# Attention probabilities turned by block transposes and a trip through DRAM instead of TensorE, in a two-layer gated cross-attention network

## The chip, the cores and the metric

The kernel runs on one core of a Trainium2 chip (TensorE for matrix products, VectorE, ScalarE, GpSimd, SyncE which issues DMAs). The metric is device time in microseconds of one launch. Everything is float32 except a bfloat16 mask bias.

## The reference

`x` is (8, 512, 512): 8 batches of 512 tokens, 512 features. The context is (8, 120, 512): 120 keys a batch. There are 16 heads of 32 features. Two layers, each a gated cross-attention and a gated feed-forward:

```python
def xattn(Q, ctx, Wq, Wk, Wv, Wo, mask=None):      # layer 1 adds biases and a key mask
    q, k, v = split_heads(Q @ Wq.T), split_heads(ctx @ Wk.T), split_heads(ctx @ Wv.T)
    scores = einsum('bhqd,bhkd->bhqk', q, k) / sqrt(32)
    if mask is not None:
        scores = where(mask == 0, -1e30, scores)
    probs = softmax(scores)                        # (8, 16, 512, 120)
    out = einsum('bhqk,bhkd->bhqd', probs, v)
    return merge_heads(out) @ Wo.T

x = x + tanh(g_xattn[0]) * xattn(layernorm(x), ctx, ...)
x = x + tanh(g_ffn[0]) * routed_ffn(layernorm(x))  # 128 experts, each takes 1 token of each 32
x = x + tanh(g_xattn[1]) * xattn(layernorm(x), ctx, ..., mask)
x = x + tanh(g_ffn[1]) * channel_mix(layernorm(x)) # two mixes with the previous token, 3 products
```

## The kernel before

The 4096 tokens are 32 tiles of 128 tokens (`NT = 32`, `TB = 4` tiles a batch). `x` stays on the chip. Both cross-attentions are the class `CrossAttention`; the work is a software pipeline of slots, one for each tile. `slot(t)` does, in program order:

- `normalize(t + 10)`: layernorm of a later tile by ScalarE; in layer 1 GpSimd also adds the output bias (`add_bias`).
- `scores(t + 1)`: 16 products (one a head) of queries and keys into two PSUM tiles `s` of 8 heads (in layer 1 first four products that add the mask), then the softmax. The heads of `s[1]` go one at a time through ScalarE: VectorE takes the largest of each head (line 674), and eight activations compute exp(s - max) and the sum of each head (677). The heads of `s[0]` go together: VectorE takes the largest (685) and subtracts it (687), one wide activation does the exponentials (688), VectorE sums (693). `norm` takes reciprocals (666) and divides on GpSimd (667), for 8 heads at a time.
- `queries`: two of the seven products that make a later batch's queries (each four matmuls, line 156; the seventh alone in every fourth slot), with their copies and sums on ScalarE, VectorE and GpSimd. I call the slot with one product the short slot.
- `output(t - 1, ...)`: the output projection of the tile before, in two parts (757), and the update of `x` (766).
- `transpose_probs(t)`: 16 TensorE transposes of the probabilities, [128 tokens, 120 keys] to [120 keys, 128 tokens] (705), into PSUM, then two copies to `prT` on the chip, one by VectorE (713), one by ScalarE (715).
- `transpose_x(t + 9)`: four transposes of a normalised tile (567) and a ScalarE copy (569).
- `attend(t)`: 16 products of values and `prT` (740), then the copy `aT` by ScalarE (748).

At the marks `after(t, stage)` the next part of the network puts its own work in: in layer 0 the routing of the feed-forward (`RoutedFfn.in_slot`: statistics, `route_norm` with a copy of `x` to DRAM and a ScalarE normalisation, `route_x`, `route_logits`), in layer 1 the statistics and, from slot 22 on, the first work of the channel mix (`ChannelMix.in_slot`). Slots 0 to 3 are the opening; `run` does slots 4 to 26; `tail` slots 27 to 32, which use `transpose_probs_late`.

What sets the order: inside `tc.manual_schedule(engines=...)` the named engines take their instructions in program order; the other engines are ordered by the framework's scheduler. In `run`, layer 0 has only TensorE in program order, layer 1 TensorE and SyncE. SyncE's queue takes DMAs in order, and a DMA that waits holds those behind it. On-chip tiles come from pools: `soft` (two buffers a name; `pr` are the probabilities, 128 x 2048), `late` (`prT`, one buffer), PSUM pools `p_s` (two buffers of two banks: the two `s` tiles or `tps`) and `p_mm` (four banks, shared in turn by query products, attention, routing, transposed x and output).

Of the kernel before, what the change touches and what calls it, by code (L numbers as in the profile page):

```python
# [28 lines left out]
EPS = 1e-5  # L29

MASKED = -(2.0**102)


class Common:
# [172 lines left out]
class CrossAttention:  # L207
# [7 lines left out]
    def __init__(  # L215
        self, cm, tc, es, ins, gate, aside, mask=None, biases=None, loads=(), then=None,
        vpool=None,
    ):
        self.cm, self.nc, self.tc, self.gate, self.then = cm, cm.nc, tc, gate, then
        self.masked, self.biased = mask is not None, biases is not None  # L220

        self.aside, self.turned = aside, not loads
        nc = cm.nc

        def pool(name, bufs, **kw):
            pool = tc.tile_pool(name=name, bufs=bufs, reuse_waits="tile", **kw)
            return es.enter_context(pool)

        self.pool = pool("at_w", 1)
        vpool = vpool or self.pool  # L230
        self.norm = pool("at_n", 2)
        self.soft = pool("at_soft", 2)
        self.p_mm = pool("at_mm", 4, space=PSUM)
        self.p_s = pool("at_s", 2, space=PSUM)
        self.wq = self.pool.tile([P, NC, D], FP, name="wq")
        self.wo = self.pool.tile([P, NC, D], FP, name="wo")
        self.kT = self.pool.tile([P, NC, B * LK], FP, name="kT")
        self.v = [vpool.tile([P, 2, D], FP, name=f"v{q}") for q in range(B // 2)]
        self.xn, self.xnT, self.qT, self.probs, self.aT = {}, {}, {}, {}, {}
        self.ops = {}  # L240
        self.biasless, self.opening = [], True

        def right(name):
            return tc.tile_pool(name=name, bufs=1, side="right", reuse_waits="tile")

        with right("at_v") as self.vp:
            with right("at_k") as self.kp:
                self.load(ins, list(loads), mask, biases)
                if self.biased:
                    self.scale_biases()  # L250
                self.project_keys()
                if self.masked:
                    self.make_mask()
            self.work = pool("at_work", 2)
            self.prologue()
        self.late = pool("at_late", 2)
# [359 lines left out]
    def queries(self, b, f):  # L616

        if f == 0:
            self.begin_queries(b)
        one = f == TB - 1 or self.opening and f == 2  # L620
        self.q7.next(1 if one else 2)
        if f == 0:
            self.sum_tokens(2)

    def scores(self, t):

        nc, soft = self.nc, self.soft  # L630
        b, i = divmod(t, TB)
        toks = slice(i * P, (i + 1) * P)
        keys = slice(b * LK, (b + 1) * LK)
# [12 lines left out]
        for hc in range(NC):  # L646
            for j in range(4):
                r = 32 * j
                nc.tensor.matmul(  # L649
                    s[j // 2][:, j % 2, hc * LK : (hc + 1) * LK],  # L650
                    self.qT[b][r : r + 32, hc, toks],
                    self.kT[r : r + 32, hc, keys],
                    start=not self.masked,
                    stop=not self.masked or hc == NC - 1,
                )
        pr = soft.tile([P, NC * S], FP, name="pr")[:, : NH * LK]
        pr = pr.rearrange("p (j h k) -> p j h k", h=NC, k=LK)
        sm = soft.tile([P, 4, NC], FP, name="sm")
        sv = [
            s[u][:, :, : NC * LK].rearrange("p j (h k) -> p j h k", k=LK) for u in range(2)  # L660
        ]
        rs = soft.tile([P, 4, NC, 1], FP, name="rs")

        def norm(js):
# [5 lines left out]
            )  # L670


        nmx = soft.tile([P, 2, NC, 1], FP, name="nmx")
        nc.vector.tensor_reduce(nmx, sv[1], AX.X, ALU.max, negate=True)  # L674
        for j in range(2):
            for hc in range(NC):
                nc.scalar.activation(  # L677
                    pr[:, 2 + j, hc, :],
                    sv[1][:, j, hc, :],
                    AF.Exp,  # L680
                    bias=nmx[:, j, hc, :],
                    accum_out=sm[:, 2 + j, hc : hc + 1],
                )
        mx = soft.tile([P, 2, NC, 1], FP, name="mx")
        nc.vector.tensor_reduce(mx, sv[0], AX.X, ALU.max)  # L685
        pv = pr[:, :2, :, :]
        nc.vector.tensor_tensor(pv, sv[0], mx.to_broadcast([P, 2, NC, LK]), ALU.subtract)  # L687
        nc.scalar.activation(pv, pv, AF.Exp)  # L688
        self.probs[t] = pr

# [3 lines left out]
            lambda: norm(slice(0, 2)),  # L694
        ]

    def transpose_probs(self, t):
        nc = self.nc
        pr = self.probs.pop(t)
        prT = self.late.tile([P, 4, NC, P], FP, name="prT", bufs=1)[:LK]  # L700
        for u in range(2):
            ps = self.p_s.tile([LK, 2, NC * P], FP, name="tps", tag="s")
            for jj in range(2):
                for hc in range(NC):
# [2 lines left out]
                        pr[:, 2 * u + jj, hc, :],  # L707
                        self.cm.ident,
                    )
            dst = prT[:, 2 * u : 2 * u + 2, :, :]  # L710
            src = ps.rearrange("p j (h t) -> p j h t", t=P)
            if u == 0:
                nc.vector.tensor_copy(dst, src)  # L713
# [4 lines left out]
    def transpose_probs_late(self, t):  # L718

        nc = self.nc  # L720
        pr = self.probs.pop(t)
        prT = self.late.tile([P, 4, NC, P], FP, name="prT", bufs=1)[:LK]
        for j in (2, 3, 0, 1):
            ps = self.p_mm.tile([LK, NC, P], FP, name="tps", tag="mm")
            for hc in range(NC):
                nc.tensor.transpose(ps[:, hc, :], pr[:, j, hc, :], self.cm.ident)
            if j % 2 == 0:
                nc.vector.tensor_copy(prT[:, j, :, :], ps)  # L728
            else:
                nc.scalar.copy(prT[:, j, :, :], ps)  # L730
        self.probs[t] = prT

    def attend(self, t):
# [3 lines left out]
        for hc in range(NC):  # L737
            for j in range(4):
                h = 4 * hc + j
                nc.tensor.matmul(  # L740
                    aps[32 * j : 32 * j + 32, hc, :],
                    self.v[b // 2][:LK, b % 2, h * HD : (h + 1) * HD],
                    prT[:, j, hc, :],
                    start=True,
                    stop=True,
                )
        self.aT[t] = self.late.tile([P, NC, P], FP, name="aT")
        nc.scalar.copy(self.aT[t], aps)  # L748

    def output(self, t, chunks):  # L750

        nc, x = self.nc, self.cm.x
        if 0 in chunks:
            self.ops[t] = self.p_mm.tile([P, D], FP, name="ops", tag="mm")
        ops = self.ops[t]
# [6 lines left out]
                stop=(c == NC - 1),  # L762
            )
        if NC - 1 in chunks:
            del self.ops[t], self.aT[t]
            nc.vector.scalar_tensor_tensor(
                x[:, t, :], ops, self.gate, x[:, t, :], ALU.mult, ALU.add
            )

    def after(self, t, stage):  # L770

# [3 lines left out]

    def run(self):
        for t in range(TB, NT - TB - 1):
            self.slot(t)

    def slot(self, t):  # L780

        if t + 10 < NT and not self.opening:
            self.normalize(t + 10)
        rest = self.scores(t + 1)
        while rest and not self.opening:
            rest.pop(0)()
        self.queries(*divmod(t + TB + 1, TB))
        self.after(t, 0)


        short = t % TB == TB - 2
        ahead = 3 if short or t == 1 else 2
        if t > 0:
            self.output(t - 1, range(ahead))
        x_ahead = short and not self.masked and not self.opening
        if x_ahead and t + 9 < NT:
            self.transpose_x(t + 9)
        if rest:
            rest.pop(0)()
        self.transpose_probs(t)  # L800
        while rest:
            rest.pop(0)()
# [2 lines left out]
            self.q7.next()  # L805
        if t > 0:
            self.output(t - 1, range(ahead, NC))
        if t + 9 < NT and not x_ahead:
            self.transpose_x(t + 9)
        if self.opening:  # L810
            self.add_bias(2)
            self.normalize(t + 10)
        self.after(t, 1)
        self.attend(t)
        self.after(t, 2)

    def tail(self):

        for t in range(NT - TB - 1, NT + 1):
            rest = self.scores(t + 1) if t + 1 < NT else []  # L820
            self.after(t, 3)
            self.after(t, 0)
# [11 lines left out]
class RoutedFfn:  # L834
# [43 lines left out]
    def route_stats(self, t):  # L878
        layernorm_sums(self.cm, self.route, t)
        layernorm_scales(self.cm, self.route, t, 1)  # L880

    def route_norm(self, t):

        nc, x = self.nc, self.cm.x[:, t, :]
        nc.sync.dma_start(out=self.aside[t * P : (t + 1) * P, :], in_=x)
        nc.scalar.activation(
            x, x, AF.Identity, bias=self.cm.nmr[:, t, :], scale=self.cm.rstd[:, t, :]
        )

    def route_x(self, t, ps):  # L890
        nc = self.nc
# [36 lines left out]
    def in_slot(self, s, attention, stage):  # L928

        last = NT - TB - 1  # L930
        if stage == 2 and 0 <= s - 1:
            self.route_stats(s - 1)
        if (stage == 2 and (0 <= s - 1 < last - 1 or s == NT)) or (stage == 3 and s > last):
# [269 lines left out]
class ChannelMix:  # L1203
# [56 lines left out]
    def in_slot(self, s, attention, stage):  # L1260

        nc = self.nc
        self.at = attention
        if stage == 2 and 0 <= s - 2 < NT - 2 * TB:
            attention.stats(s - 2)
        if stage == 2 and s == NT - 1:
            for c in range(NC):
# [256 lines left out]
def flamingo_kernel(ctx: ExitStack, tc: tile.TileContext, a: dict, out: bass.AP):  # L1524
# [25 lines left out]
    with ExitStack() as es:  # L1550
# [5 lines left out]
        with ExitStack() as at:  # L1556
            with tc.manual_schedule(engines=every):
# [3 lines left out]
                    vpool=ffn.vpool,  # L1561
                )
                attention.first_slots()
            with tc.manual_schedule(engines={engines.PE}):
                attention.run()
            with tc.manual_schedule(engines=compute):
                attention.tail()
# [1 line left out]
    with ExitStack() as es:  # L1569
# [3 lines left out]
        with tc.manual_schedule(engines=every):  # L1573
# [2 lines left out]
                gates[:, 1:2], aside, a["mask"], (a["bqk"], a["bv"], a["bo"]), then=mix.in_slot,  # L1576
            )
            attention.first_slots()
        with tc.manual_schedule(engines={engines.PE, engines.SP}):
            attention.run()  # L1580
        with tc.manual_schedule(engines=compute):
            attention.tail()
# [64 lines left out]
```

## Time and profile before

| | |
|---|---|
| median of 3 runs | 1404.27 us (1403.76 to 1408.66) |
| the profiled execution | span 1402.0 us, from its first to its last instruction |
| TensorE matmul busy | 1363.8 us, 97% |
| VectorE, ScalarE, GpSimd busy | 1051.7 (75%), 761.8 (54%), 698.9 us (50%) |
| DMA | 71.45 MB in 46010 packets, nearly all in the loads at the start and in the feed-forward of layer 0 |
| the chain that ended last, by engine | TensorE 71%, VectorE 15%, ScalarE 5%, GpSimd 5% |

The slots of layer 0 run from about 85 to 410 us, those of layer 1 from about 750 to 1045 us. The chain is the sequence of work that ended last: each piece was waited for by the next. A group's row gives the line, the engine, the operation, the tile written and the tiles read, shapes, count, busy time, mean duration of one, and the idle time of the engine just before it with what ended it. `PEld` is TensorE's weight load, which runs beside its products.

### The profile page before, as it was taken

How to read it: one execution, taken by the hardware profiler on the slowest of the kernel's cores; microseconds unless marked ns; L12 is line 12 of the kernel's file. 1: busy time of each engine (PE TensorE's matmuls, PEld its weight loads, DVE VectorE, ACT ScalarE, POOL GpSimd, SP SyncE). 2: the span in 40 equal slices, each digit the busy share in tenths (PEclk: the TensorE clock that was granted, in tenths of full speed). 3: DMA queues.
4: the chain of work that ended last, by engine and by line, in shares of the span. 5: the costliest groups of instructions: out<-in, count | busy, mean ns of one | idle time of the engine just before them, and what ended most of it. 6: DMA issues, size and time to landing. Idle time of an engine off the chain costs nothing.

```text
span 1402.0 us, 32996 instructions
## 1 busy us (share of the span) xinstructions
PE 1363.8 (97%) x13888; PEld 1099.8 (78%) x13888; DVE 1051.7 (75%) x1498; ACT 761.8 (54%) x1860; POOL 698.9 (50%) x620
## 2 busy tenths in 40 slices
PE   7999999999999998999999999999999999999997
PEld 6887777777777787888888777777766888888886
DVE  4876767777777777777887777777777678877776
ACT  1366666666666445445136666665665655544543
POOL 4855545555444001555797766565548244343341
PEclk9999999999999999999999999999999999999999
DMA  9500000000001347431410000000000000000001
GB/s 297 184 8 25 17 23 24 24 24 24 18 30 47 130 133 240 123 107 61 148 61 2 2 1 2 1 2 2 1 32 2 0 31 30 31 31 31 30 22 40
DMA packets 46010, 71.45 MB, mean 51 GB/s; under 512 B 2926, under 2 KB 22894, under 8 KB 45862
## 3 DMA queue, kind: packets, MB, share of 16 engines
q1 hardware_dynamic: 45573, 69.34, 15.0%
q8 instruction: 109, 1.79, 0.5%
q14 instruction: 40, 0.32, 0.1%
q10 hardware_dynamic: 288, 0.00, 0.0%
HBM read 50.59 MB, written 18.74 MB: 49 GB/s over the span
## 4 chain that ended last, share of the span: by engine, by line
PE 71%; DVE 15%; ACT 5%; POOL 5%; issue 3%; DMA 1%; SPq 0%; POOLq 0%; DVEq 0%; ACTq 0%
PE ops L757 15%; PE qps L156 14%; PE tps L705 7%; PE cps L156 5%; PE aps L740 4%; PE s L649 4%; PE rps L1164 3%; PE vps L156 2%; PE rlps L903 2%; PE l1ps L1079 2%; PE ops L1185 2%; PE xnps L567 2%; PE gps L1052 2%; DVE cv L1428 2%; DVE xr L1353 2%
## 5 line engine op out<-in xcount | busy, mean ns | idle before, releaser
L667 POOL TENSOR_TENSOR pr<-pr,rs 128x960 f32<-128x960 f32 x128 | 230.1, 1800 | 236.2 <-DVE rs L666 225.7
L757 PE MATMUL ops<-wo,aT 128*128 128x512 f32 x512 | 239.7, 594 | 0.7 <-ACT aT L748 0.7
L677 ACT ACTIVATE pr<-s,nmx 128x120 f32<-128x120 f32 x512 | 176.3, 372 | 84.9 <-DVE nmx L674 72.0
L757 PEld LDWEIGHTS ops<-wo,aT 128*128 128x128 f32 x512 | 92.3, 190 | 71.8 <-issue 66.9
L1177 POOL TENSOR_TENSOR r<-r,b 128x1024 f32<-128x1024 f32 x31 | 73.5, 2377 | 141.5 <-ACT r L1176 141.5
L156 PE MATMUL qps<-xnT,wq 128*128 128x256 f32 x512 | 121.3, 384 | 0.0
L705 PEld LDWEIGHTS tps<-ident,pr 128*120 128x120 f32 x864 | 96.8, 138 | 28.5 <-issue 24.9
L677 ACT ACTIVATION_READ_ACCUMULATOR pr<-s,nmx 128x1 f32 x512 | 111.8, 218 | 0.0
L685 DVE TENSOR_REDUCE mx<-s 128x8 f32<-128x960 f32 x64 | 73.9, 1154 | 47.8 <-PE s L649 47.8
L156 PEld LDWEIGHTS qps<-xnT,wq 128*128 128x128 f32 x512 | 94.6, 189 | 15.2
L705 PE MATMUL tps<-ident,pr 128*120 128x128 f32 x864 | 104.4, 273 | 1.4 <-ACT pr L677 1.3
L49 DVE BATCH_NORM_STATS2 bnst<-x 128x6 f32<-128x512 f32 x128 | 87.5, 684 | 1.3
L693 DVE TENSOR_REDUCE sm<-pr 128x8 f32<-128x960 f32 x64 | 73.1, 1142 | 18.9 <-ACT pr L688 18.6
L674 DVE TENSOR_REDUCE nmx<-s 128x8 f32<-128x960 f32 x64 | 73.6, 1150 | 11.2 <-PE s L649 11.2
L1431 POOL TENSOR_TENSOR x<-x,cv 128x512 f32<-128x512 f32 x28 | 41.4, 1479 | 70.7 <-DVE cv L1428 70.7
L715 ACT COPY prT<-tps 120x1024 f32<-120x1024 f32 x54 | 54.9, 1016 | 38.9 <-PE tps L705 38.7
L687 DVE TENSOR_TENSOR pr<-s,mx 128x960 f32<-128x960 f32 x64 | 73.7, 1151 | 1.8 <-DVE mx L685 0.5
L740 PE MATMUL aps<-prT,v 120*32 120x128 f32 x2048 | 70.4, 276 | 1.5 <-DVE prT L728 1.2
L649 PE MATMUL s<-kT,qT 32*128 32x120 f32 x2048 | 71.1, 276 | 0.0
L649 PEld LDWEIGHTS s<-kT,qT 32*128 32x128 f32 x2048 | 65.7, 186 | 6.6 <-issue 6.4
L713 DVE COPY prT<-tps 120x1024 f32<-120x1024 f32 x54 | 65.4, 1211 | 3.5 <-PE tps L705 3.5
L569 ACT ACTIVATE xnT<-xnps 128x512 f32<-128x512 f32 x64 | 38.6, 603 | 53.7 <-PE xnps L567 53.7
(231 smaller groups left out, 3178.1 us busy)
## 6 DMA issues: line engine op xcount, KB each, us to landing
w<-in_w_dram SPq DMA_DIRECT2D x32, 512.0 KB, 4.7
x<-in_x_dram SPq DMA_DIRECT2D x8, 1024.0 KB, 16.1
aside<-x SPq DMA_DIRECT2D x32, 256.0 KB, 2.0
x<-aside SPq DMA_DIRECT2D x8, 1024.0 KB, 10.7
out_dram<-x SPq DMA_DIRECT2D x14, 512.0 KB, 2.8
wk<-in_wk_dram SPq DMA_DIRECT2D x3, 1024.0 KB, 7.5
wv<-in_wv_dram SPq DMA_DIRECT2D x3, 1024.0 KB, 5.4
wq<-in_wq_dram SPq DMA_DIRECT2D x2, 1024.0 KB, 14.0
```

The costliest lines, as they stand in the source:

```text
L49: cm.nc.vector.bn_stats(st, cm.x[:, t, :])
L156: self.nc.tensor.matmul(ps[:, m, :], rows[:, k, m * n : (m + 1) * n], columns[:, k, :], start=(k == 0), stop=(k == 1),)
L649: nc.tensor.matmul(s[j // 2][:, j % 2, hc * LK : (hc + 1) * LK], self.qT[b][r : r + 32, hc, toks], self.kT[r : r + 32, hc, keys], start=no ...
L667: nc.gpsimd.tensor_tensor(pr[:, js, :, :], pr[:, js, :, :], rs[:, js, :, :].to_broadcast([P, 2, NC, LK]), ALU.mult,)
L674: nc.vector.tensor_reduce(nmx, sv[1], AX.X, ALU.max, negate=True)
L677: nc.scalar.activation(pr[:, 2 + j, hc, :], sv[1][:, j, hc, :], AF.Exp, bias=nmx[:, j, hc, :], accum_out=sm[:, 2 + j, hc : hc + 1],)
L685: nc.vector.tensor_reduce(mx, sv[0], AX.X, ALU.max)
L687: nc.vector.tensor_tensor(pv, sv[0], mx.to_broadcast([P, 2, NC, LK]), ALU.subtract)
L705: nc.tensor.transpose(ps[:, jj, hc * P : (hc + 1) * P], pr[:, 2 * u + jj, hc, :], self.cm.ident,)
L740: nc.tensor.matmul(aps[32 * j : 32 * j + 32, hc, :], self.v[b // 2][:LK, b % 2, h * HD : (h + 1) * HD], prT[:, j, hc, :], start=True, stop ...
L757: nc.tensor.matmul(ops, self.aT[t][:, c, :], self.wo[:, c, :], start=(c == 0), stop=(c == NC - 1),)
L1177: nc.gpsimd.tensor_tensor(r, r, b2, ALU.add)
```

## The change

For tiles 4 to 25 of each layer (`CROSSED`, 22 tiles) the probabilities are no longer transposed by TensorE:

- The exponentials of all 16 heads go one head at a time, with their sums (the subtraction 687, the wide exponential 688 and the sum 693 are no longer used there). They are written in another layout: for each half of 8 heads, key `4 f + k` of head `h` lies at column `k * 256 + h * 32 + f` (`KB = 4`, `KF = 30`; columns `f` = 30 and 31 are padding, set to zero once by GpSimd). GpSimd divides as before, in this layout.
- `turn_blocks(t, u)`: VectorE transposes the half (128 x 1024) in place in blocks of 32 x 32, and SyncE writes it to DRAM as four planes of 128 x 256 (512 KB).
- `fetch_blocks(t, u)`: four DMAs, one for each plane, read it back so that partition `4 f + k` of `prT` holds the probabilities of key `4 f + k`, for the tokens in four groups of 32.
- `attend` reads `prT` in that layout: 32 tokens at a time from four places.

`run` calls the new `steady(t)` instead of `slot(t)`, with all five engines in program order in both layers. Its order differs from `slot`: the products of the scores, the update of `x` from two slots before, both largest values, the first half's exponentials with one query product between them, the block transpose of half 0 of tile t, the attention of tile t - 1 (one slot later than before), the reads of tile t, the second half's exponentials, the second query product, the transposition of x, the block transpose of half 1 of tile t + 1, the output of tile t - 1 in one piece. The routing of layer 0 is split and partly one slot later. Slot 26, whose tile is not crossed, uses `transpose_probs_late` and `attend` at once. `slot` now serves the opening alone.

```diff
+KB, KF = 4, 30
+CROSSED = range(TB, NT - TB - 2)
...
+    def softmax(self, t, sv):
...
+        def largest(u):
+            nc.vector.tensor_reduce(nmx[u], sv[u], AX.X, ALU.max, negate=True)
+
+        def exponentials(u, js=(0, 1)):
+            for j in js:
+                for hc in range(NC):
+                    src = sv[u][:, j, hc, :]
+                    if crossed:
+                        dst = half[u][:, :, NC * j + hc, :].rearrange("p k f -> p f k")
+                        src = src.rearrange("p (f k) -> p f k", k=KB)
+                    else:
+                        dst = half[:, u, NC * j + hc, :]
+                    nc.scalar.activation(
+                        dst, src, AF.Exp, bias=nmx[u][:, j, hc, :],
+                        accum_out=sm[:, u, j, hc : hc + 1],
+                    )
+
+        def divide(u):
+            nc.vector.reciprocal(rs[:, u], sm[:, u])
+            by = rs[:, u].rearrange("p j h -> p (j h)")
+            if crossed:
+                by = by.unsqueeze(1).unsqueeze(3).to_broadcast([P, KB, 2 * NC, KF])
+                nc.gpsimd.tensor_tensor(half[u], half[u], by, ALU.mult)
...
+    def turn_blocks(self, t, u):
+        nc = self.nc
+        pr = self.probs[t][:, u * 1024 : (u + 1) * 1024]
+        nc.vector.transpose(pr, pr)
+        plane = self.dram.tile([KB, P, 256], FP, name=f"plane{u}")
+        nc.sync.dma_start(
+            out=plane.rearrange("k p e -> p k e"),
+            in_=pr.rearrange("p (k e) -> p k e", k=KB),
+        )
+        self.planes[t, u] = plane
+
+    def fetch_blocks(self, t, u):
+        if u == 1:
+            del self.probs[t]
+            self.probs[t] = self.late.tile([P, 2, 4, 256], FP, name="prT", bufs=1)
+        plane = self.planes.pop((t, u))
+        for k in range(KB):
+            self.nc.sync.dma_start(
+                out=self.probs[t][k : LK : KB, u, :, :],
+                in_=plane[k].rearrange("(q f) e -> f q e", q=4)[:KF],
+            )
...
+                if t in CROSSED:
+                    at = (NC * (j % 2) + hc) * 32
+                    p = prT[:LK, j // 2, :, at : at + 32]
+                    out = out.rearrange("p (q t) -> p q t", q=4)
...
+    def steady(self, t):
+        b, f = divmod(t + TB + 1, TB)
+        sv = self.score_products(t + 1)
+        self.after(t, 4)
+        if t - 2 in self.ops:
+            self.add_output(t - 2)
+        if t + 10 < NT:
+            self.normalize(t + 10)
+        self.after(t, 5)
+        largest, exponentials, divide = self.softmax(t + 1, sv)
+        largest(1)
+        largest(0)
+        exponentials(1, (0,))
+        if f == 0:
+            self.begin_queries(b)
+        if f != TB - 1:
+            self.q7.next()
+        exponentials(1, (1,))
+        if t in CROSSED:
+            self.turn_blocks(t, 0)
+        divide(1)
+        if t > TB:
+            self.attend(t - 1)
+        if t in CROSSED:
+            self.fetch_blocks(t, 1)
+        self.after(t, 0)
+        self.after(t, 1)
+        exponentials(0)
+        self.after(t, 6)
+        self.q7.next()
+        if f == 0:
+            self.sum_tokens(2)
+        if t in CROSSED:
+            self.fetch_blocks(t, 0)
+        else:
+            self.transpose_probs_late(t)
+        if t + 9 < NT:
+            self.transpose_x(t + 9)
+        if t + 1 in CROSSED:
+            self.turn_blocks(t + 1, 1)
+        divide(0)
+        self.output(t - 1, range(NC), later=True)
+        if t not in CROSSED:
+            self.attend(t)
...
     def in_slot(self, s, attention, stage):
         last = NT - TB - 1
+        if stage == 5:
+            if s - 3 >= TB - 1:
+                self.route_scale(s - 3)
+            if s - 2 >= TB - 1:
+                self.put_aside(s - 2)
+        if stage == 6 and s - 2 >= TB - 1:
+            self.route_stats(s - 2)
...
-            with tc.manual_schedule(engines={engines.PE}):
+            with tc.manual_schedule(engines=every):
                 attention.run()
...
-        with tc.manual_schedule(engines={engines.PE, engines.SP}):
+        with tc.manual_schedule(engines=every):
             attention.run()
```

## The prediction

> **What bounds the kernel now.** I read the busy table by stretches first, over one batch (four slots) of each attention layer, 302.15 to 351.69 us and 857.86 to 902.19 us (columns: stretch, its length, then busy us of TensorE matmul, weight load, VectorE, ScalarE, GpSimd, then granted clock, DMA share, GB/s):
>
> ```profile
> 302.15:351.69 49.54, 49.54 (x478) 38.14 (x477) 35.52 (x57) 32.36 (x95) 25.31 (x26) 1.00 0.06 22
> 857.86:902.19 44.33, 44.33 (x443) 32.74 (x441) 32.90 (x46) 27.35 (x87) 27.65 (x23) 1.00 0.01 1
> ```
>
> TensorE is busy all the time, at full clock; the others have at least a quarter free and DMA is idle. So a slot's length is the sum of its TensorE pieces, which the chain of waits gives (start, length, what) for one slot of layer 0:
>
> ```profile
> 312.03 1.10 PE s L649 x32
> 313.13 3.65 PE qps L156 x16
> 316.78 1.72 PE ops L757 x4
> 318.50 1.75 PE tps L705 x16
> 320.25 1.72 PE ops L757 x4
> 321.96 0.44 PE xnps L567 x4
> 322.40 0.89 PE rlps L903 x8
> 323.29 0.44 PE rxps L894 x4
> 323.73 1.01 PE aps L740 x32
> ```
>
> They add to 12.71 us without a gap. The 16 transposes of probabilities (L705) are 1.75 of it. A slot with one query product instead of two (every fourth) is 1.82 shorter. In layer 1 a slot is 11.48 (no routing pieces; a mask product of 0.21 more).
>
> Last, the groups that the change touches (busy us, mean ns of one | idle before):
>
> ```profile
> L705 PE MATMUL tps<-ident,pr 128*120 128x128 f32 x864 | 104.4, 273 | 1.4 <-ACT pr L677 1.3
> L667 POOL TENSOR_TENSOR pr<-pr,rs 128x960 f32<-128x960 f32 x128 | 230.1, 1800 | 236.2 <-DVE rs L666 225.7
> L688 ACT ACTIVATE pr<-pr 128x960 f32<-128x960 f32 x64 | 66.8, 1043 | 0.0
> L715 ACT COPY prT<-tps 120x1024 f32<-120x1024 f32 x54 | 54.9, 1016 | 38.9 <-PE tps L705 38.7
> L713 DVE COPY prT<-tps 120x1024 f32<-120x1024 f32 x54 | 65.4, 1211 | 3.5 <-PE tps L705 3.5
> 304.44 0.36 ACT L677 ACTIVATE pr<-s,nmx 128x120 f32<-128x120 f32 x1 [2.10 <-DVE nmx L674]
> 304.79 0.35 ACT L677 ACTIVATE pr<-s,nmx 128x120 f32<-128x120 f32 x1
> ```
>
> The last two lines, from the timeline, show that exponentials of single heads follow each other every 0.34 us (eight in 2.74), although the accumulator read between them is booked separately.
>
> **What goes.** Of 64 tiles, 44 (tiles 4 to 25 of both layers) lose their transposes: 44 x 1.75 = 77 us of a TensorE that never waits there. That is the ceiling: 1402 - 77 = 1325 on the span. With them go L713 on VectorE (1.21), and by the head-by-head exponentials the subtraction L687 (1.15) and the sum L693 (1.14); on ScalarE L715 (1.02) and L688 (1.04).
>
> **What comes, per slot.** ScalarE: eight more single-head exponentials, 8 x 0.34 = 2.74; net +0.7. They now write one element every 1 KB. The nearest rows with scattered writes are the ScalarE copies L1069 (1012 ns, as the plain L715) and L1146 (1121 ns); bounds 0.34 to, if the 0.80 ns per element between L677 and L688 doubled, 0.45 each; I take 0.34. VectorE: two block transposes of 1024 elements, no such row. Lower bound 0.69 (L49, 512 elements read from the same memory), upper 2.4 (two passes at L713's 1.21); I take 1.2, the copy of equal size. VectorE is then 8.9 - 3.5 + 2.4 = 7.8 per slot, and with 2.4 each 10.2, still under the slot. GpSimd: the division has the same 960 elements in runs of 30; 1.80, at most 2.23 (960 at L1177's 2377 ns for 1024). Its total stays near 6.5.
>
> SP gets ten new DMAs a slot: two writes of 512 KB in 1 KB runs, and eight reads of 120 KB. They are queued in the order write 0 of tile t, four reads of half 1, four reads of half 0, write 1 of tile t+1, so a late write 0 holds the four reads behind it. Rows:
>
> ```profile
> out_dram<-x SPq DMA_DIRECT2D x4, 256.0 KB, 2.2
> GB/s 0 0 0 0 0 0 0 0 0 0 0 109 358 345 62 0 0 0 102 355 335 82 0 0 0 89 345 358 82 0 0 0 72 355 355 92 0 0 0 0
> 680.31 0.38 SPq L312 DMA_DIRECT2D mrow<-in_mask_dram  x1
> 680.75 0.41 SPq L315 DMA_DIRECT2D gbo<-in_bo_dram  x1
> ```
>
> The first two (the last 10 us, 1 KB runs) show 256 KB landing in 2.2 us and 350 GB/s while moving. So 512 KB lands in 2.2 + 0.75 = 2.9; a slot's 2.0 MB take 5.8 of some 10.5 us. The last two show issues 0.44 apart. Small loads land in 1.6 to 2.6 (rows bqk, bc); a 120 KB read: 2.1. From the end of a block transpose to the last byte in place: 2.9 + 4 x 0.44 + 2.1 = 6.7. Upper bound: 5 for the write and 6 for the reads (as the 512 KB and 960 KB loads that met others, 4.7 and 6.5), 11.
>
> [...]
>
> **The new slot, layer 0**, from its start. TensorE: scores to 1.10, product 2.93, attend (of the tile before) 3.94, routing 5.27, product 7.09, x 7.53, output 10.97. VectorE: the late x update, maxima 1.2 to 3.5, product addition or not, block transpose to 4.7 or 5.4. ScalarE: half 1 from 2.45, a query copy (0.6) in two slots of four, to 5.2 or 5.8, attention copy (0.58), routing copy, half 0 done at 9.1 or 9.7, before the next scores want the banks. Where one product is missing, TensorE is at 5.27 when it needs the bank that the attention copy frees at 5.77: 0.5 lost. A batch saves 7.0 - 0.5 = 6.5. With 22 tiles, 5.5 batches: 36 us.
>
> **Layer 1.** TensorE would end at 9.73, or 7.90 in the short slot. But the output needs the attention copy, which is queued on ScalarE behind half 1: at 5.87, plus 0.6 or 0.9 in slots with a query copy. TensorE is there at 6.29, so 0.2 and 0.5 lost; in the short slot at 4.47, 1.4 lost. A batch saves 7.0 - 2.1 = 4.9; 5.5 batches 27 us. Slots 22 to 25 also have the channel mix's normalisation (0.81) and copy (0.59) in the ScalarE queue between the exponentials: -4.
>
> **The trip.** Block transpose at 4.7 plus 6.7 gives 11.4; attend of the next slot wants it at 10.97 + 2.93 = 13.9, after a short slot at 9.6 + 2.93 = 12.6, before a short slot (block transpose at 5.4, so 12.1) at 12.1 in layer 0 and 10.9 in layer 1, where the wait for the attention copy hides it. So DMA is covered with 0 to 2.5 us; 3 us for what misses it. Slot 26 transposes and attends at once as the tail does: -1.5 in each layer.
>
> Sum: 36 + 27 - 4 - 3 - 3 = 53. Span 1402.0 - 53 = 1349; the median of the runs is 2.3 above the span: **1351 us**.
>
> **Rivals.**
> - *ScalarE becomes the bound.* Scores need all 16 exponentials of the last tile done. At 0.45 each the loop scores, maximum, exponentials, copies is 10.5 to 11.4 in layer 1 and 10.9 to 11.5 in layer 0: savings of 5 and 26 us, less 7: **1380**. For: the loop is only about 1 us below TensorE's. Against: L1069.
> - *Slower: the trip through DRAM.* If it takes 13 us instead of 6.7, every second slot waits at attend: 14.7 and 14.8 us. A batch is then 48.9 against 44.3 and 51.5 against 49.5: +25 and +11, and +6 from the ends: **1446**. It decides from about 11.5 on, the upper bound. For: there is one landing buffer (prT), nothing in the trace shows a write and a read of the same DRAM in a loop, and SP must issue in order. Against: DMA is idle now, and its rows are half of that.
> - *No change*: the 77 us become waits between engines, since all five now run in a written order where TensorE alone (layer 0) did before, about 1404. Against: every queue above has slack.
>
> **Numbers.** Forecast 0.57 (own range 1332 to 1370), ScalarE or a half-late trip 0.16, no change 0.05, slower 0.22. A measurement of this kernel can tell 0.5% (7 us) from no change. Faster 0.73, same 0.05, slower 0.22. The range runs from just under the ceiling, 1404 - 77 - 5 = 1322, to 1418, where a trip of about 12 us lies; beyond is most of the slower rival.
>
> **What would show it.** Right: the 16-transpose pieces gone from the chain in the slots, batches of 43.0 and 39.5 us, single-head exponentials still 0.34 apart, block transposes near 1.2, DMA share near 0.55 in the slots. Wrong: TensorE idle before attend with a DMA as releaser (trip), before scores with ScalarE (loop), or VectorE's block transposes of 2 us and more with GpSimd waiting.

## The result and the profile after

| | before | changed kernel |
|---|---|---|
| median of the runs beside each other | 1404.91 us (1403.76 to 1408.66, 4 runs) | 1426.13 us (1422.50 to 1428.86, 4 runs) |
| span of the profiled execution | 1402.0 us | 1426.8 us |
| mean granted TensorE clock | 0.999 | 0.979 |

The ratio is 1.0149, with a 95% interval of 1.0127 to 1.0171: the changed kernel is 1.5% slower, where 3.8% faster was forecast (1351 us, range 1322 to 1418). The time lies outside the range and on the other side.

The busy table by stretches of the changed kernel, one batch of each layer as before (stretch, its length, busy us of TensorE matmul, weight load, VectorE, ScalarE, GpSimd, then granted clock, DMA share, GB/s):

```profile
219.46:266.08 46.62, 44.39 (x413) 31.35 (x412) 32.14 (x53) 35.53 (x151) 25.44 (x27) 1.00 0.61 200
867.78:914.75 46.97, 41.68 (x380) 27.86 (x377) 28.91 (x43) 30.50 (x143) 27.67 (x23) 0.93 0.54 174
```

Batches are 46.6 and 47.0 us where 43.0 and 39.5 were forecast and 49.5 and 44.3 were before. TensorE is no longer busy throughout: 2.2 and 5.3 us of a batch are idle, and in layer 1 its clock is 0.93. The DMA share is the forecast one.

The groups that the change touches, on the page (busy us, mean ns of one | idle before):

```profile
L716 POOL TENSOR_TENSOR pr<-pr,rs 128x960 f32<-128x960 f32 x88 | 159.5, 1814 | 149.1 <-DVE rs L712 129.7
L850 PE MATMUL aps<-prT,v 120*32 120x128 f32 x2048 | 84.2, 291 | 41.9 <-DMA prT<-plane 33.1
L778 DVE STREAM_TRANSPOSE pr<-pr 128x1024 f32<-128x1024 f32 x88 | 108.9, 1238 | 6.3 <-POOL pr L716 5.3
```

The division and the block transpose cost what was forecast (1.81 and 1.24 us). The attend products (L850) now have 41.9 us of idle time ahead of them, 33.1 of it ended by a landing of prT: the sign that the prediction had named for a wrong trip. The DMA rows of the page (KB each, median us to landing), and the reads' own line from the view of that source line (ns min/median/max of one issue):

```profile
plane<-pr SPq DMA_DIRECT2D x88, 512.0 KB, 3.1
prT<-plane SPq DMA_DIRECT2D x352, 120.0 KB, 2.7
```
```profile
L793 SPq DMA_DIRECT2D prT<-plane x352: 822/823/1831, 137.4 to 1053.9; - x176
```

Landings were forecast well enough (2.9 and 2.1). The issue of one read takes SyncE 0.82 us, and they start 0.87 apart; 0.44 was forecast. What that makes of the trip, in the chain of waits for one slot of layer 1 (start, us, what):

```profile
860.86 1.15 DVE pr L778
862.01 0.21 DVE rs L712
862.22 0.18 SPq L780
...
862.69 0.86 SPq L793
...
863.60 0.85 SPq L793
...
867.96 0.82 SPq L793
...
868.83 3.29 DMA prT<-plane
872.12 0.14 issue
872.25 2.15 PE aps L850 x31
874.41 2.00 PE qps L159 x4
```

From the end of the block transpose (862.0) to the last byte (872.1) it is 10.1 us: 0.7 to the first read, seven read issues 6.1, and the landing of the eighth read, which the profile counts from the start of its issue, 3.3. In a slot of layer 0 (block transpose ends at 201.60, last byte at 211.01) it is 9.4. TensorE's own timeline over the same stretch (start, us, instruction, in brackets the idle time before it):

```profile
860.54 1.30 PE L850 MATMUL aps<-prT,v 120*32 120x128 f32 x32 [0.84 <-DVE nmx L695]
861.77 1.99 PE L159 MATMUL qps<-xnT,wq 128*128 128x256 f32 x8
...
872.25 2.15 PE L850 MATMUL aps<-prT,v 120*32 120x128 f32 x32 [3.42 <-DMA prT<-plane]
...
874.34 3.78 PE L159 MATMUL qps<-xnT,wqs 128*128 128x256 f32 x8
```

After an idle time of 3.42 us the attend takes 2.15 us instead of 1.3, and the query product 3.78 instead of 1.99. The busy table for that stretch (same columns as above) gives a granted clock of 0.53:

```profile
872.25:878.47 6.22, 6.21 (x44) 5.00 (x45) 1.30 (x5) 4.21 (x23) 1.81 (x1) 0.53 0.53 180
```

At 0.53 of the clock the 6.2 us hold some 2.9 us more than at full clock (an estimate, 6.2 x 0.47). In this slot the wait is paid almost twice.

Where the time went, from the starts of the score products in the two timelines (us between the starts of the tiles named; "steady" stretches lie wholly among slots with the trip; the few products of tiles 28 and 60 that run far ahead in the changed kernel, shown below, are not taken as their starts):

| stretch | before | changed | difference |
|---|---|---|---|
| layer 0, tiles 4 to 6 (into the crossed slots) | 26.0 | 35.3 | +9.3 |
| layer 0, tiles 6 to 26 (steady) | 246.4 | 236.4 | -10.0 |
| layer 0, tiles 26 to 28 (out of them) | 23.3 | 30.6 | +7.3 |
| layer 1, tiles 36 to 40 | 44.3 | 47.0 | +2.7 |
| layer 1, tiles 40 to 58 (steady) | 200.4 | 206.3 | +5.9 |
| layer 1, tiles 58 to 60 | 21.3 | 28.2 | +6.9 |

The sum is +22.1. So there are two losses: the 38 steady slots, which were to bring some 48 us (36 + 27 - 4 - 3 = 56 for 44 slots), bring 4; and the four places where the kernel goes into and out of the crossed slots cost 26.2.

### The profile page after: what moved, and what is told of

Its sections match the earlier page's. It is cut to its first block, busy times and chain, and to the rows that moved or that the text cites. A ratio compares the mean times of both kernels' runs of the same rounds, so it can differ in the third digit from the quotient of the medians.

```text
span 1426.8 us, 33176 instructions
## 1 busy us (share of the span) xinstructions
PE 1329.8 (93%) x13184; PEld 1040.3 (73%) x13184; DVE 1004.1 (70%) x1448; ACT 800.4 (56%) x2538; POOL 701.2 (49%) x624
## 4 chain that ended last, share of the span: by engine, by line
PE 53%; DVE 16%; SPq 8%; ACT 6%; DMA 6%; POOL 5%; issue 5%; POOLq 0%; DVEq 0%; ACTq 0%
PE ops L867 10%; PE qps L159 10%; SPq L793 7%; PE aps L850 5%; PE cps L159 5%; DMA prT<-plane 4%; PE rps L1346 3%; PE s L651 3%; PE rlps L1074 2%; PE vps L159 2%; PE l1ps L1261 2%; PE ops L1367 2%; ACT pr L706 2%; DVE rT L1326 2%; DVE cv L1610 2%
## 5 line engine op out<-in xcount | busy, mean ns | idle before, releaser
L706 ACT ACTIVATE pr<-s,nmx 128x120 f32<-128x120 f32 x768 | 279.2, 494 | 142.0 <-issue 73.1
L706 ACT ACTIVATION_READ_ACCUMULATOR pr<-s,nmx 128x1 f32 x768 | 192.6, 251 | 0.0
L850 PE MATMUL aps<-prT,v 120*32 120x128 f32 x2048 | 84.2, 291 | 41.9 <-DMA prT<-plane 33.1
L695 DVE TENSOR_REDUCE nmx<-s 128x8 f32<-128x960 f32 x96 | 106.7, 1153 | 19.9 <-PE s L651 19.9
L778 DVE STREAM_TRANSPOSE pr<-pr 128x1024 f32<-128x1024 f32 x88 | 108.9, 1238 | 6.3 <-POOL pr L716 5.3
L850 PEld LDWEIGHTS aps<-prT,v 120*32 120x32 f32 x2048 | 63.5, 115 | 66.5 <-issue 40.5
L881 DVE SCALAR_TENSOR_TENSOR x<-ops,gates,x 128x512 f32<-128x512 f32 x64 | 47.8, 746 | 87.6 <-PE ops L867 86.7
L159 PE MATMUL qps<-xnT,wqs 128*128 128x256 f32 x256 | 68.7, 415 | 0.0
L1358 ACT COPY r<-rps 128x1024 f32<-128x1024 f32 x31 | 31.4, 1013 | 59.1 <-PE rps L1346 59.1
L1346 PE MATMUL rps<-ident,rT 128*128 128x128 f32 x512 | 61.9, 275 | 1.8 <-DVE rT L1326 1.4
L1346 PEld LDWEIGHTS rps<-ident,rT 128*128 128x128 f32 x512 | 55.5, 141 | 7.5 <-issue 4.8
## 6 DMA issues: line engine op xcount, KB each, us to landing
x<-aside SPq DMA_DIRECT2D x8, 1024.0 KB, 10.4
```

Of the source, the lines that this page charges most:

```text
L159: self.nc.tensor.matmul(ps[:, m, :], rows[:, k, m * n : (m + 1) * n], columns[:, k, :], start=(k == 0), stop=(k == 1),)
L695: nc.vector.tensor_reduce(nmx[u], sv[u], AX.X, ALU.max, negate=True)
L706: nc.scalar.activation(dst, src, AF.Exp, bias=nmx[u][:, j, hc, :], accum_out=sm[:, u, j, hc : hc + 1],)
L778: nc.vector.transpose(pr, pr)
L850: nc.tensor.matmul(out, self.v[b // 2][:LK, b % 2, h * HD : (h + 1) * HD], p, start=True, stop=True,)
L1346: nc.tensor.transpose(ps[:, k // 4, (k % 4) * P : (k % 4 + 1) * P], self.rT[:, 16 * tq + 8 * h + k, :], self.cm.ident,)
```

## The experiments

The theory (A): the way over DRAM sets the slot, through SyncE, which issues eight reads one after the other at 0.87 us. It binds in two ways. In a row: the block transpose ends 4.7 to 5.4 us after the slot's start; 0.6 + 7 x 0.87 + 2.7 = 9.4 to the last byte; less the 2.93 at which attend stands, that is a slot of 11.2 to 11.9. In a loop: there is one landing buffer, so the reads can only leave when attend has read it, and attend 1.3 + 7 x 0.87 + 2.7 is 10.1 and more where a landing is late. (The expectations count eight issues ahead of the landing where the profile has seven, so their rows are 0.6 to 0.9 too long.) Rivals: transfers (B: landings, or the landing buffer alone), ScalarE's exponentials (C), the new order by itself.

**Reads of 32 partitions.** All else stays; the two padding rows of each block are fetched too.

```diff
-                out=self.probs[t][k : LK : KB, u, :, :],
-                in_=plane[k].rearrange("(q f) e -> f q e", q=4)[:KF],
+                out=self.probs[t][k : P : KB, u, :, :],
+                in_=plane[k].rearrange("(q f) e -> f q e", q=4),
```

> Edit: each read of a plane takes 32 rows instead of 30 (the two padding rows too), so 128 KB instead of 120 KB and 32 partitions instead of 30; nothing else. Theory A (SyncE's issue time): the 352 reads of 30 partitions occupy SyncE 0.82 to 0.85 us each, the 128-partition writes 0.36, and eight of them in a row, between the end of one attend and the start of the next, make the loop of the landing buffer about 11 us. If 32 partitions are issued like 128, a read costs about 0.4 us, the loop falls by some 3.5 us below TensorE's own 9.7 to 11, slots go to about 11.1 (layer 0) and 10.3 (layer 1): 1370 to 1390 us. Theory B (landing time and bytes): issue time does not change, or does not matter; bytes rise by 7%: 1426 to 1435 us. Theory C (the halved clock after idle stretches is its own cause): the waits stay and so does the clock of 0.979.

Measured: 1394.66 us (1394.26 to 1396.22), ratio 0.9928 (0.9913 to 0.9943), 31 us less than the changed kernel and faster than before. The reads' line and the landings in this kernel:

```profile
L793 SPq DMA_DIRECT2D prT<-plane x352: 577/604/1730, 136.4 to 1020.8; - x176
```
```profile
plane<-pr SPq DMA_DIRECT2D x88, 512.0 KB, 3.3
prT<-plane SPq DMA_DIRECT2D x352, 128.0 KB, 2.7
```

The issue fell from 0.82 to 0.60 while bytes rose by 7% and the landing stayed at 2.7; the idle time of attend on landings fell from 33.1 to 17.6 us. So SyncE's time for issuing is on the path, and 7% more bytes cost nothing that can be seen. The time lies 5 us above the 1370 to 1390 that A expected.

**The new order with TensorE's transposes**, no trip at all:

```diff
-CROSSED = range(TB, NT - TB - 2)
+CROSSED = range(0)
...
-        if t > TB:
+        if t - 1 in CROSSED:
             self.attend(t - 1)
```

> Edit: the set of crossed tiles is empty, so the new slot order and the head-by-head exponentials stay, and all tiles are transposed by TensorE as before; no block transposes, no trip through DRAM. Theory A (the trip is what costs): TensorE gets its 77 us back and does not wait for DMA; about the time of the kernel before plus what the order costs at the ends of the stretch and by late transposes, 1404 to 1420 us, clock 1.0 in the slots. Rival (the written order of all engines is what costs): slots are no better than in the changed kernel although no DMA is waited for: above 1430 us.

Measured: 1501.58 us (1499.51 to 1502.76), ratio 1.0682 (1.0664 to 1.07). A's 1404 to 1420 failed, and the number lies where the rival wanted it, above 1430. But the edit also brings back the transposes in the written order and attend in the tile's own slot, so it does not separate the trip from the order. TensorE's transposes wait 46.7 us in all for VectorE's query additions (qT). In one slot these stand in VectorE's written order behind the reciprocal that waits for the exponentials, and from 200 to 216 us ScalarE's exponentials (L706) are 32.3% of the chain. As a test of the theory it was a miss. What speaks against the rival are the kernels with a shorter trip, above and below: they keep the written order of all engines in the slots and are faster than before.

**The block transpose of half 0 ahead of the second row maximum**, with reads of 30 and then of 32 partitions:

```diff
         largest(1)
+        if t in CROSSED:
+            self.turn_blocks(t, 0)
         largest(0)
         exponentials(1, (0,))
...
         exponentials(1, (1,))
-        if t in CROSSED:
-            self.turn_blocks(t, 0)
         divide(1)
```

> The changed kernel with one move: the block transpose of half 0 and its write stand between the two row maxima instead of behind both, so that write 0 can leave about 1.1 to 1.2 us earlier in the slot (one row maximum); the reads stay at 30 partitions and 0.87 us apart. Theory A (the way over DRAM, in its row 'block transpose, write, eight reads in SyncE's queue, landing', sets the slot): the row starts 1.1 to 1.2 earlier, and steady slots fall from 11.8 / 11.5 to about 10.9, where the loop over the one landing buffer takes over (attend 1.0 to 1.3, eight issues of 0.87, landing 2.7 = 10.9): 2 x 22 x 0.6 to 0.9 = 26 to 40 us less than the changed kernel, 1388 to 1400 us. Theory B (the loop over the one landing buffer sets the slot already, attend's end to the next landing): the write's start is not on it, no gain: 1420 to 1428 us. Theory C (ScalarE's exponentials set the slot): the second half's maximum comes 1.2 us later, so no gain or a loss, 1426 to 1450 us.

> Both moves together: reads of 32 partitions (issues 0.65 apart) and the block transpose of half 0 between the two row maxima. Theory A: the row is 3.5 + 0.4 + 8 x 0.65 + 2.7 = 11.8 after the slot's start, less the 2.93 at which attend stands: slots of at least 8.9; the loop over the landing buffer 1.0 + 5.2 + 2.7 = 8.9 too. Both lie under TensorE's own 10.97 / 9.73, so TensorE's work sets the slot again (means about 10.7 and 10.0): against the 32-row kernel's 1394.7 some 0.3 x 44 = 13 us less, 1378 to 1386 us. Theory B gives the same bound here and tells nothing apart. Theory C (ScalarE): no gain over the 32-row kernel, 1392 to 1400 us.

Measured: with 30 partitions 1406.17 us (1401.89 to 1411.07), ratio 1.0005 (0.9992 to 1.0017); with 32 partitions 1378.38 us (1375.57 to 1380.57), ratio 0.9809 (0.9789 to 0.9829). So one edit at a time brings 20 and 31 us, both together 48. The first lies between the expectations of A (1388 to 1400) and B (1420 to 1428), the second where A had it. SyncE's timeline in the 30-partition kernel says why the early write alone brings less, with TensorE's beside it:

```profile
857.78 2.18 SPq L780 DMA_DIRECT2D plane<-pr  x2
861.41 6.94 SPq L793 DMA_DIRECT2D prT<-plane  x8
...
891.29 2.03 SPq L780 DMA_DIRECT2D plane<-pr  x2
894.73 6.94 SPq L793 DMA_DIRECT2D prT<-plane  x8
```
```profile
860.03 1.33 PE L850 MATMUL aps<-prT,v 120*32 120x128 f32 x32 [2.95 <-DMA prT<-plane]
...
893.39 1.31 PE L850 MATMUL aps<-prT,v 120*32 120x128 f32 x32 [0.93 <-DVE pr L778]
```

The writes have been issued (857.78 + 2.18), yet the reads leave only at 861.41 and 894.73, 0.05 and 0.03 us after attend ends: the loop over the one landing buffer has taken over from the row. Each late attend makes the next reads late; from 893.39 to the next attend at 904.76 it is 11.4 us. With issues 0.65 apart that loop is 1.3 + 7 x 0.65 + 2.7 = 8.6 us, under TensorE's own slot, and the idle time of attend on landings, from the view of waits (us in total, times, longest), goes from 33.1 us to

```profile
PE aps L850 <- DMA prT<-plane: 3.6, 5, 1.6
```

in the kernel with both edits. Rival C falls with it: the exponentials are the same, and the slots are short.

**What the issue time hangs on.** The keys of a head are split into runs of 30 instead of every fourth key, so that a read lands on partitions side by side; and the same with 32 rows.

```diff
-                        dst = half[u][:, :, NC * j + hc, :].rearrange("p k f -> p f k")
-                        src = src.rearrange("p (f k) -> p f k", k=KB)
+                        dst = half[u][:, :, NC * j + hc, :]
+                        src = src.rearrange("p (k f) -> p k f", k=KB)
...
-                out=self.probs[t][k : LK : KB, u, :, :],
+                out=self.probs[t][k * KF : (k + 1) * KF, u, :, :],
```

> The changed kernel with the keys of a head split into four runs of 30 instead of every fourth, so that each read lands on 30 partitions side by side (rows 30k to 30k+29) instead of on every fourth partition; bytes, reads, waits and order stay. It asks what the 0.82 us of SyncE for one read hang on. Theory 'the step of four between the landing partitions': the issue falls to about 0.4 and the time to the TensorE-bound 1375 to 1390 us. Theory 'the count of 30': the issue stays at 0.82 and the time at 1420 to 1430 us (the exponentials now write and read their runs in line, which moves nothing if 0.34 us apart stays).

> The 32-partition kernel with its reads landing side by side (rows 32k to 32k+31). The part left out: the values are still taken from rows 0 to 119 in the old order, so keys and values are not matched and the result is not the reference's; every instruction, byte and wait is there. Theory 'the step of four': issue about 0.4, against 0.60 with the step. Theory 'the count alone': 0.60 stays. Time 1380 to 1396 us.

Measured: 30 rows 1391.73 us (1390.73 to 1393.49), ratio 0.99 (0.9884 to 0.9917); 32 rows 1390.27 us (one run). The issue, first with 30, then with 32 partitions side by side:

```profile
L793 SPq DMA_DIRECT2D prT<-plane x352: 315/414/1566, 137.2 to 1015.6; - x176
```
```profile
L793 SPq DMA_DIRECT2D prT<-plane x352: 302/432/1989, 136.5 to 1014.1; - x176
```

It is 0.41 and 0.43 against 0.82 and 0.60 with the step of four: here the step costs, and the count matters only with the step. The time, though, is within 5 us of the kernel with 32 partitions and the step (1394.66). The chain of waits of the 30-partition kernel, in one slot of layer 0, shows what came in its place:

```profile
194.72 2.76 ACT pr L706 x15
197.47 3.23 DMA plane<-pr
...
200.72 0.32 SPq L793
...
201.08 0.41 SPq L793
...
201.54 0.41 SPq L793
...
201.99 3.62 DMA prT<-plane
...
205.71 1.30 PE aps L850 x32
```

The four reads of half 1 are issued before write 0 has landed, so the landing of the write (3.2 us) has taken the place of their issues, and the last read lands 3.6 us after its issue where it was 2.7: 3.2 + 1.3 for three issues + 3.6 = 8.1, against 0.6 + 7 x 0.65 + 2.7 = 7.9 worked out for 32 partitions and the step. The expected 1375 to 1390 left out that new wait.

**The ends.** In the changed kernel the way out of the crossed slots looks like this on TensorE:

```profile
397.01 1.17 PE L651 MATMUL s<-kT,qT 32*128 32x120 f32 x32
402.39 0.78 PE L651 MATMUL s<-kT,qT 32*128 32x120 f32 x4 [4.21 <-ACT pr L706]
403.10 1.94 PE L850 MATMUL aps<-prT,v 120*32 120x128 f32 x32
404.96 2.08 PE L1074 MATMUL rlps<-rxT,wc 128*128 128x128 f32 x8
```

Four score products of tile 28 stand ahead of the attend of slot 26. They wait for ScalarE to be done with the bank (4.21 us), everything behind them on TensorE waits with them, and then runs slowly (attend 1.94 instead of 1.3, logits 2.08 instead of 1.16; the granted clock is 0.53 from 402.39 to 407.40 us). The last steady slot and the tail are two written orders, one behind the other, and these products came across the seam. One order for both (shown for layer 0, and the same in layer 1):

```diff
             with tc.manual_schedule(engines=every):
                 attention.run()
-            with tc.manual_schedule(engines=compute):
                 attention.tail()
```

> The kernel with both moves (32-partition reads, early block transpose), and the last crossed slots and the tail written into one hand-set order instead of two that follow each other, in both layers; nothing is computed differently. In the two-part order the first score products of tile 28 stand on TensorE ahead of the attend of slot 26 and wait 4.2 us for the exponentials that free their bank, and the matmuls behind the wait run at half speed. Theory 'the exits are lost to that order': the wait of 4.2 and the 2.5 to 3.5 of slow matmuls go, in each of two layers: 10 to 16 us less than 1378, 1362 to 1368 us, and the start-to-start time of the last slots falls to TensorE's own. Theory 'the exits are bound by something else (the landing of the tile put aside, the way of tile 25 over DRAM)': another wait takes its place, 1373 to 1380 us.

Measured (with the two edits above): 1370.13 us (1366.86 to 1372.71), ratio 0.9746 (0.9723 to 0.977), 8 us less. The wait is gone from the view of waits in both layers, and tiles 26 to 28 took 24.4 instead of 30.4 us, tiles 58 to 60 24.1 instead of 28.1. That is 10 of the 10 to 16 expected; in the profiled execution the slots into layer 0 took 4.5 us more than in the one compared with, from the same instructions in the same order there.

The way in, in the changed kernel, on SyncE, ScalarE and TensorE:

```profile
131.96 0.37 SPq L780 DMA_DIRECT2D plane<-pr  x1
132.38 0.50 SPq L1046 DMA_DIRECT2D aside<-x  x1
```
```profile
137.43 0.81 ACT L1052 ACTIVATE x<-x,nmr,rstd 128x512 f32<-128x512 f32 x1 [3.62 <-DMA aside<-x]
138.15 0.44 ACT L706 ACTIVATE pr<-s,nmx 128x120 f32<-128x120 f32 x1
138.48 0.45 ACT L706 ACTIVATE pr<-s,nmx 128x120 f32<-128x120 f32 x1
```
```profile
140.14 0.65 PE L573 MATMUL xnps<-ident,xn 128*128 128x128 f32 x4 [1.81 <-ACT xnT L186]
141.99 6.52 PE L867 MATMUL ops<-wo,aT 128*128 128x512 f32 x8 [1.20 <-ACT rxT L1067]
```

The 256 KB that are put aside are queued behind the 512 KB of the first crossed half and land 5 us later; ScalarE waits 3.62 us for that, with the exponentials and copies behind it; TensorE waits for the copies, and its output product takes 6.52 instead of 3.60, at a granted clock of 0.56. A slot earlier, 16 exponentials stand ahead of the copies of tile 3's transposed probabilities. Both reordered:

```diff
+            largest(1)
+            exponentials(1)
+            largest(0)
+            rest = [lambda: divide(1), lambda: exponentials(0), lambda: divide(0)]
...
+            self.transpose_probs_late(t)
...
-        if t + 1 in CROSSED:
-            self.turn_blocks(t + 1, 1)
         self.after(t, 1)
         self.attend(t)
         self.after(t, 2)
+        if t + 1 in CROSSED:
+            self.turn_blocks(t + 1, 1)
...
-            if s - 3 >= TB - 1:
+            if s - 3 >= TB - 2:
                 self.route_scale(s - 3)
...
+            if s == TB - 1:
+                self.put_aside(s - 1)
+            else:
+                self.route_norm(s - 1 if stage == 2 else s - 2)
```

> The same, and the slot that leads into the crossed ones reordered: tile 3's probabilities are transposed between the two halves of tile 4's exponentials (into the four small PSUM banks) instead of behind all 16, the tile put aside is written ahead of the 512 KB write of the first crossed half, and its scale by ScalarE moves to the slot in which it is wanted; nothing is computed differently. Theory 'the entry is lost to ScalarE's queue (16 exponentials and a wait for a landing ahead of what TensorE needs)': slots 3 and 4 of the first layer fall from 18.6 + 12.2 to about 14 + 12, those of the second from 12.5 + 8.7 + 10.6 little: 3 to 7 us less than the kernel with the exit alone, 1356 to 1364 us if that one is at 1365. Theory 'the entry is bound by the first way over DRAM': less than 2 us either way.

Measured: 1361.85 us (1360.08 to 1363.87), ratio 0.9689 (0.9665 to 0.9712), 8 us less again; tiles 4 to 6 take 26.9 us (35.3 in the changed kernel, 26.0 before). The busy table by stretches of this kernel, one batch of each layer:

```profile
205.20:249.21 44.01, 43.58 (x413) 30.58 (x412) 31.97 (x53) 35.42 (x152) 25.50 (x27) 1.00 0.66 215
835.48:876.01 40.53, 39.08 (x380) 25.70 (x376) 28.64 (x43) 30.36 (x144) 27.84 (x23) 1.00 0.64 209
```

TensorE is busy for 43.6 of 44.0 us and 39.1 of 40.5, at full clock: it sets the slot again.

**A shorter trip still**: the same kernel with reads of 30 partitions side by side (the edit shown above).

> The kernel with early block transpose, joined exit and reordered entry, with the reads on 30 partitions side by side (issues of 0.41 instead of 0.60). If TensorE's own work sets the slots there already, a way over DRAM that is shorter by 8 x 0.1 us is worth nothing more: 1358 to 1364 us, and the idle TensorE has on landings stays at some 4 us. If the way over DRAM still set slots, 1350 to 1357.

Measured: 1361.15 us (1360.32 to 1361.52), ratio 0.9688 (0.9671 to 0.9705): no difference, as expected where the trip is hidden already. Attend's idle time on landings is 3.3 us.

## Why the prediction was wrong

**The step that failed** is the trip, "2.9 + 4 x 0.44 + 2.1 = 6.7". Two things in it were off above all, and both are SyncE's.
- The duration: 0.44 between two issues was read from loads for the second cross-attention (680.31 and 680.75 us); a read of 30 partitions with a step of four takes 0.87. Those loads have another shape, and the prediction gave an upper bound for the landings only, none for the issue. The 0.44 is also the least of the five distances in that row of loads, which run to 0.66 (from 679.02 to 681.81 us).
- The count: the prediction wrote down the queue (write 0, four reads of half 1, four of half 0) and noted that a late write 0 holds the four reads behind it, and then counted only the last four. Behind write 0 stand eight issues, seven of them ahead of the last read, and half 1's reads could not go long before, because the one landing buffer is free only after attend. With 0.6 + 7 x 0.87 in place of 2.9 + 4 x 0.44, and 2.7 for the read, the sum is 9.4; 9.4 and 10.1 were measured in the two slots named.

The duration is the larger part. In the prediction's own sum it is worth 4 x 0.43 = 1.7 us; the landing of a read, 2.7 for 2.1, adds 0.6, and the count only the last 0.3. With issues of 0.44 the whole queue would have been 0.6 + 7 x 0.44 + 2.7 = 6.4, no more than was forecast.

What was taken from it, "DMA is covered with 0 to 2.5 us; 3 us for what misses it", failed with it: a trip longer by 2.7 to 3.4 us is later than that slack in every slot, and the steady slots gained 4 us in place of 48. The prediction's own sum shows the size: 4.7 to 5.4 plus 9.4 less 2.93 is 11.2 to 11.9 a slot, and 11.8 in layer 0 and 11.5 in layer 1 were measured, against 12.3 and 11.1 before (steady stretches over 20 and 18 tiles). The gap between layers follows: layer 0 gains 0.5 a slot, layer 1 loses 0.3. In layer 1 it is only the mean that agrees: the slots with two query products take 10.4 to 11.6 us and the short one 12.9 to 14.4, because there attend comes right behind the scores and meets the wait (3.0 to 3.6 us, and a granted clock of 0.50 to 0.82 in the 1.7 to 2.2 us behind it).

**The slower rival** was the right one in its mechanism and its sign, but it was priced by a trip of 13 us and was to decide "from about 11.5 on". The trip was 9.4 to 10.1, and by the prediction's own slack that is late in every slot, so 11.5 was set too high. At that length the steady slots together still gain 4 us; it is with the ends that the sum turns. With a shorter trip alone (1378.38 us, ends as they were) the kernel is faster than before; the ends repaired with the long trip were not tried.

**The ends** were 3 us in the sum ("slot 26 transposes and attends at once as the tail does: -1.5 in each layer") and cost 26.2. The way in had no term at all, and neither had two things that the diff showed: the write put ahead of the tile put aside in SyncE's queue, with ScalarE waiting for that landing, and the 16 exponentials ahead of tile 3's copies. That products of the tail move across the seam of two written orders was not considered; TensorE's order in the trace shows it.

**The clock** had no term either. The price of a wait was taken as the wait; after the waits shown, of 3.4 and 4.2 us, it was the wait and, behind it, 6.2 and 5.0 us of matmuls at a granted clock of 0.53 (from 872.25 and from 402.39 us).

**What held.** Transposes on TensorE are gone, and with the trip and the ends repaired the batches are 44.0 and 40.5 us against the forecast 43.0 and 39.5: the gain from TensorE's pieces was right to 1 us a batch. Block transpose 1.24 (1.2 forecast), division 1.81 (1.80), DMA share 0.61 and 0.54 (0.55). Exponentials of single heads with scattered writes still start 0.34 apart, so the ScalarE rival is out:

```profile
119.31 0.45 ACT L706 ACTIVATE pr<-s,nmx 128x120 f32<-128x120 f32 x1
119.64 0.46 ACT L706 ACTIVATE pr<-s,nmx 128x120 f32<-128x120 f32 x1
119.98 0.47 ACT L706 ACTIVATE pr<-s,nmx 128x120 f32<-128x120 f32 x1
```

(Their durations grew from 0.36 to 0.45 and more, their distance did not.) The repaired kernel is 42 us faster than before where 53 was forecast: 44 of the difference in the steady stretches (27.3 in layer 0, 16.3 in layer 1), and its ends cost 3.

## What to carry to other kernels

Count the issues of a DMA queue as work with a duration of its own, for the exact shape and step of the transfer (0.41 to 0.82 us for one read here), and count all that stand between the write and the last read, not only those that carry the late data. Where a buffer has one copy, add up its loop (reader, issues, landing) beside the row that fills it; shortening one of them can hand the slot to the other (here the shorter row alone brought 20 us, and the loop then set the slot). Look at the slots that lead into and out of a rewritten stretch with the same care as at the stretch: a queue that changes its order there can cost as much as the stretch gains.

## What the runs showed of the hardware

- SyncE's time to issue one DMA differed with its shape (medians): 0.82 us for 30 partitions with a step of four, 0.60 for 32 with that step, 0.41 and 0.43 for 30 and 32 side by side, 0.37 for the 512 KB write of 128 partitions. What in the issue makes the step costly was not tried.
- With issues 0.46 apart, on partitions side by side, a read landed in 3.3 us (median); with the step of four and issues 0.65 to 0.87 apart in 2.7, for about the same bytes. Whether the step or the closer issues do it was not tried.
- After TensorE had been idle for 3.42 us, the granted clock was 0.53 for the next 6.2 us in the slot shown. After 4.21 us of idle time it was 0.53 for the next 5.0 us (402.39 to 407.40).
- Shorter waits had a lower clock behind them too, and their length alone did not decide it. In the changed kernel attend took 2.13 us at 304.41 us after a wait of 2.00 (clock 0.57) and 1.30 at 814.84 us after a wait of 2.60 (clock 1.00). Before the output product at 141.99 us there were two waits of 1.81 and 1.20 with 0.65 of work between them; its 6.52 us had a granted clock of 0.56.
